# Down projection of a gated feed-forward block in 2x2 blocks with seven products, and its weights checked through an int8 copy

## The chip, the cores and the metric

The kernel runs on one core of a Trainium2 chip. The metric is device time in microseconds (us), lower is better. A core has a matrix engine (PE, with weight loads in its own row PEld), a vector engine (DVE), an activation engine (ACT), a general engine (POOL) and a queue engine (SP) that mostly issues transfers (DMA) between the chip's memory and the core's on-chip memory (SBUF). Matrix products are summed in eight banks (PSUM) of 128 x 512 float32 numbers each.

## The reference, cut to what matters

The kernel computes a transformer block with adaptive layer norms for 2 sequences of 1024 tokens, 1024 wide, in float32. The part that the change touches is the feed-forward block at the end, with 2752 inner channels. Its three weight matrices hold only -1, 0 and 1:

```python
def _L0_ffn_ref(x, Wg, Wu, Wd, ag, au, ad):
    gate = jnp.einsum('bsh,ih->bsi', x, Wg) * ag
    up = jnp.einsum('bsh,ih->bsi', x, Wu) * au
    h = jax.nn.silu(gate) * up
    out = jnp.einsum('bsi,hi->bsh', h, Wd) * ad
    return out
...
x = x + ga * _L0_attn_ref(...)
h = _layernorm(x, axis=-1) * (1 + cb) + sb
x = x + gb * _L0_ffn_ref(h, ...)
```

## The kernel before, in words

The stages follow each other: modulation vectors, QKV projections, attention, output projection (all of it until about 1409 us), then the **gate and up pass** (1409 to 2019 us), then the **down projection** (2019 to 2346 us) and a short tail. Below, n is a number of rows, P is 128, b the sequence, and D is 1024.

Precise products: the weights are small integers and exact, so only the token side is split into a rounded part `hi` and the rest `lo`, and each product is two passes over TensorE, `hi` and `lo`.

**Gate and up pass** (`gate_up`, from L1636). For each of two sequences it runs over 11 groups p of 256 inner channels (the last has 192). A group is multiplied in 2x2 blocks with seven products in place of eight: the tuple `SEVEN` (L768) names for each product e the output half (x or y: its PSUM bank), the left operand (a block or a sum S1 to S4 of blocks of the weights), the right one (of the tokens, `hs_tiles`, made earlier and resident), and the block sum to which it adds. A product is 8 matmuls 128x512 for gate and 8 for up; a group is 112 matmuls. Around them:
- `stage` (L1508) loads the weights of the next group into two buffers of the pool `wst`, four transfers of 512 KB on SP.
- `weight_operands` (L1602) makes the seven left operands: casts A11, A12, A22 on ACT (L1611, L1612, L1617) and four sums on POOL (L1613 to L1616).
- `ternary` (L1561) checks the raw weights with two DVE passes 2048 wide (L1570 counts entries that are neither what 0 or 1 gives, L1573 counts the -1), into `count_a` and `count_b`. Gate and up weights are checked once: in sequence 0 from group 1 on, group 0 in sequence 1.
- The down weights are checked on the way too (`down_checks`, L1634): a piece of 1 MB per group is loaded into a `wst` buffer (`wdst`), checked, and stored to `wd_dram`. One lies in the last group of sequence 0, ten in sequence 1.
- Products leave PSUM by an ACT copy (L1661), a DVE addition (L1666), `silu` on ACT (L1676) and the product with up on DVE (L1679). The activation goes to memory (`act_dram`) in pieces of 256 KB, four per group, on SP.
- At the start of sequence 1 its seven token operands are loaded (`tokens_in`, L1524: a 1 MB transfer through the two `traw` buffers, an ACT cast L1528, a DVE subtraction L1529), behind sequence 0's last uses.

From the second group on, PE follows the order of the program (`pinned`); other engines' orders are set by a scheduler, each engine executing its own queue in order. Checks stand behind the latest PSUM read (`hold`, L1554).

**Down projection** (from L1692). All weights (11 pieces) stay in SBUF, loaded at its start from `wd_dram` by SP's and ACT's queues (L1705). For each of 16 tiles of 128 tokens, an activation row block `a` is loaded on ACT's queue (L1713), cast to `hi` on ACT (L1722), and `lo` is the difference on DVE (L1723); two sets of these buffers alternate. 88 matmuls (22 channel blocks, hi and lo, two halves of the output) fill two banks; then DVE multiplies by the gate (L1742), POOL adds the residual `x1` (L1743), and SP stores. 1408 matmuls in all. Two probes (`exact`, L1577) and the `verdict` (L1342) stand in this stage: if the weights aren't what the fast path needs, a slow general path runs at the end.

Of the kernel before, what the change touches and what calls it, by code (L numbers as in the profile page):

```python
# [19 lines left out]
P = 128  # L20
# [460 lines left out]
def kernel(  # L481
# [35 lines left out]
    count_b = flag.tile([P, NCOUNT + 2], FP, name="count_b")  # L517
    nc.vector.memset(count_b, 0.0)
# [46 lines left out]
    wd_dram = [dram.tile([P, 2, D], FP, tag=f"wd_{p}", name=f"wd_{p}") for p in range(NPR)]  # L565
    act_dram = [dram.tile([P, NJ, 2, NIC, P], FP, tag=f"act_{b}", name=f"act_{b}") for b in range(B)]
# [775 lines left out]
    def verdict(pool, psp):  # L1342


        seen = pool.tile([P, NCOUNT + 2], FP, name="seen")
        nc.vector.tensor_sub(seen, count_a, count_b)
        total = pool.tile([P, 1], FP, name="total")
        nc.vector.tensor_reduce(total, seen, mybir.AxisListType.X, ALU.add)
        nc.vector.tensor_scalar(total, total, 0.0, None, ALU.is_equal)
        nc.vector.tensor_mul(total, total, fine)  # L1350
        lows = psp("lows")[0:1, 0:P]
        transpose(lows, total, ident)
        least = pool.tile([1, 1], FP, name="least")
        nc.vector.tensor_reduce(least, lows, mybir.AxisListType.X, ALU.min)
        bad = pool.tile([1, 1], FP, name="bad")
        nc.vector.tensor_scalar(bad, least, 1.0, None, ALU.is_lt)
        nc.vector.tensor_copy(bad_i, bad)
# [133 lines left out]
    def share(a):  # L1491
# [11 lines left out]
    stp, wsp, ptp = (  # L1503
        gu.enter_context(tc.tile_pool(name=n, bufs=k, side="right", reuse_waits="tile"))
        for n, k in (("wst", 2), ("wops", 1), ("fpart", 1))
    )

# [53 lines left out]
    def ternary(w, at, pool):  # L1561


        junk = pool.tile([P, 2048], mybir.dt.bfloat16, tag="junk", name=f"junk_{at}")
        n = w.shape[0]
        shape = list(w.shape[1:])
        j = junk[0:n, 0 : int(np.prod(shape))]
        if len(shape) > 1:
            j = j.rearrange("p (a b) -> p a b", a=shape[0])
        hold(nc.vector.scalar_tensor_tensor(  # L1570
            j, w, 0.0, w, ALU.is_gt, ALU.not_equal, accum_out=count_a[0:n, at : at + 1]
        ))
        hold(nc.vector.tensor_scalar(  # L1573
            j, w, -1.0, None, ALU.is_equal, ALU.add, accum_out=count_b[0:n, at : at + 1]
        ))

    def exact(t, at, bank, pool):  # L1577


        matmul(bank, ident_r, t, start=True, stop=True)  # L1580
        junk = pool.tile([P, 2048], mybir.dt.bfloat16, tag="junk", name=f"probe_{at}")[:, 0:512]
        nc.vector.scalar_tensor_tensor(
            junk, bank, 1.0, t.bitcast(FP), ALU.mult, ALU.not_equal, accum_out=count_a[:, at : at + 1]
        )

    if True:
# [10 lines left out]
        with gu:  # L1597
            W_ORDER = ("A11", "A12", "S2", "S1", "S3", "S4", "A22")

            token_tiles([5, 6])  # L1600

            def weight_operands(p, st, b):  # L1602
# [5 lines left out]
                W = {q: wsp.tile([P, 2, KC // 2, P], FR, tag=f"w{q}", name=f"w{q}_{b}_{p}") for q in W_ORDER}  # L1608
# [9 lines left out]
                if b == (p == 0):  # L1618
                    for kh in range(2):
                        v = st[kh].rearrange("p a k f -> p (a k) f")[:, :, 0 : 2 * n]  # L1620
                        ternary(v, 2 * p + kh, jkp)
                return W

            down_checks = ({NPR - 1: [0]}, {p: [p + 1] for p in range(NPR - 1)})

            def gate_up(b):
# [5 lines left out]
                for p in range(NPR):  # L1632
# [4 lines left out]
                    for p_ in down_checks[b].get(p, ()):  # L1637
                        r0, n = PAIRS[p_]
                        t = stp.tile([P, 2, D], FP, tag="wst", name=f"wdst_{p_}")
                        nc.sync.dma_start(t[0:n], wd_t[ds(r0, 2 * n), :].rearrange("(m p) e -> p m e", p=n))  # L1640
                        ternary(t[0:n].rearrange("p m e -> p (m e)"), 2 * NPR + p_, jkp)
                        nc.sync.dma_start(wd_dram[p_][0:n], t[0:n])
                    n = PAIRS[p][1]
                    if p + 1 < NPR or b + 1 < B:
                        st.append(stage((p + 1) % NPR))
                    bank = {(mat, c_): ffbank(f"{mat}{c_}_{b}_{p}") for mat in "gu" for c_ in "xy"}
                    part = {}
                    for e, (c_, qa, qb_, q) in enumerate(SEVEN):
                        done = {}
# [18 lines left out]
                        if q in QUAD:  # L1668
# [13 lines left out]
                            if q == "U6":  # L1682
                                last_read[0] = ins
                            nc.sync.dma_start(
                                act_dram[b][0:n, :, h, ib, :], u[0:n].rearrange("p (j t) -> p j t", j=NJ)
                            )
# [5 lines left out]
        with ExitStack() as dn:  # L1692
            aip = [own(dn, f"ain{i}") for i in range(2)]
            lop0, hip0, hip1, lop1, gbp = (own(dn, n) for n in ("alo0", "ahi0", "ahi1", "alo1", "gb"))
            wdp = [own(dn, f"wd{p}") for p in range(NPR)]
            xp1, yp = own(dn, "x1in", 2), own(dn, "yout", 2)
            hip, lop = (hip0, hip1), (lop0, lop1)
            dlp = jkp
            wd = [wdp[p].tile([P, 2, D], FR, tag=f"wd{p}", name=f"wd_{p}") for p in range(NPR)]
            gb = []  # L1700

            def more_wd(which):
                for p in which:
                    n = PAIRS[p][1]
                    (nc.scalar if 0 < p < 8 else nc.sync).dma_start(wd[p][0:n].bitcast(FP), wd_dram[p][0:n])  # L1705

            n1 = PAIRS[-1][1]
            for b in range(B):
                for j in range(NJ):
                    for h in range(2):  # L1710
                        t = 2 * j + h
                        a = aip[h].tile([P, NIC, P], FP, tag=f"ain{h}", name=f"a_{b}_{t}")
                        nc.scalar.dma_start(a[:, 0:WHOLE], act_dram[b][:, j, h, 0:WHOLE])  # L1713
                        nc.scalar.dma_start(a[0:n1, WHOLE:NIC], act_dram[b][0:n1, j, h, WHOLE:NIC])
                        hi = hip[h].tile([P, NIC, P], FR, tag="ahi", name=f"hi_{b}_{t}")
                        lo = lop[h].tile([P, NIC, P], FR, tag="alo", name=f"lo_{b}_{t}")
                        cuts = [0, 4, 10, WHOLE] if (b, t) == (0, 0) else [0, WHOLE]
                        for v in (
                            *((slice(0, P), slice(u, w)) for u, w in zip(cuts, cuts[1:])),
                            (slice(0, n1), slice(WHOLE, NIC)),  # L1720
                        ):
                            nc.scalar.copy(hi[v[0], v[1]], a[v[0], v[1]])  # L1722
                            nc.vector.tensor_sub(lo[v[0], v[1]], a[v[0], v[1]], hi[v[0], v[1]].bitcast(FP))  # L1723
                        if (b, t) == (0, 0):
                            more_wd(range(NPR))
                            for b_ in range(B):
                                gb.append(gbp.tile([P, D], FP, name=f"gb{b_}"))
                                nc.scalar.dma_start(gb[b_], gate_dram[5][b_].partition_broadcast(P))
                        pss = [ffbank(f"dn_{b}_{t}_{n}") for n in range(2)]
                        for ib in range(NIC):  # L1730
                            rows = PAIRS[ib // 2][1]
                            for s_, src_ in enumerate((hi, lo)):
                                for n in range(2):
                                    matmul(
                                        pss[n], src_[0:rows, ib, :], wd[ib // 2][0:rows, ib % 2, ts(n, HALF)],
                                        start=(ib == 0 and s_ == 0), stop=(ib == NIC - 1 and s_ == 1),
                                    )
                        x1 = xp1.tile([P, D], FP, tag="x1", name=f"x1_{b}_{t}")
                        nc.sync.dma_start(x1, x1_dram[b * NT + t])
                        y = yp.tile([P, D], FP, tag="y", name=f"y_{b}_{t}")  # L1740
                        for n in range(2):
                            nc.vector.tensor_mul(y[:, ts(n, HALF)], pss[n], gb[b][:, ts(n, HALF)])  # L1742
                            nc.gpsimd.tensor_add(y[:, ts(n, HALF)], y[:, ts(n, HALF)], x1[:, ts(n, HALF)])  # L1743
                            nc.sync.dma_start(out[b, ts(t, P), ts(n, HALF)], y[:, ts(n, HALF)])
                        if (b, t) == (0, 0):
                            for i, src_ in enumerate((hi, lo)):
                                exact(
                                    src_[:, 0:4].rearrange("p k t -> p (k t)"), NCOUNT + i, ffbank(f"probe{2 + i}"), dlp
                                )
                        if (b, t) == (1, 2):  # L1750
                            verdict(dlp, ffbank)


# [51 lines left out]
```

## Time and profile before

| What | us |
| --- | --- |
| median of 3 runs (2354.20 to 2360.12) | 2358.19 |
| the profiled execution's own time | 2356.1 |
| its span | 2354.4 |
| PE busy | 2198.6 |
| DVE busy | 1266.9 |
| POOL busy | 886.8 |
| ACT busy | 841.8 |
| gate and up pass, first matmul to first of down | about 1409 to 2019 |
| down projection, first matmul to last | 2019.36 to about 2345.9 |

How to read it: the span is that of the profiled execution, all times within it count from its start. PE is busy 93% of it, so time goes where PE waits or where it has less to do. PE's records overlap by their pipelining; the distance of their starts is what a matmul costs. "PEclk" is the clock granted to PE (1.00 is full). The mean granted clock of this execution was 0.979.

### The profile page before, as it was taken

The numbers are of one execution on the slowest core, as the hardware profiler recorded it, in microseconds if no ns is written. First come the engines' busy times: TensorE is split into PE (matmuls) and PEld (weight loads), VectorE is DVE, ScalarE is ACT, GpSimd is POOL, SyncE is SP. The second block draws the span as 40 slices with busy tenths as digits, with TensorE's granted clock in tenths as the row PEclk, the third lists the DMA queues.
The fourth block names the chain that finished last, engine by engine and source line by source line (L and its number), as shares of the span: only waits on it lengthen the run. The fifth ranks groups of instructions, "written<-read, shape, count | busy, mean of one in ns | idle before, by whom it ended". The sixth has DMA issues, their size and how long they took to land.

```text
span 2354.4 us, 26878 instructions
## 1 busy us (share of the span) xinstructions
PE 2198.6 (93%) x9713; PEld 1211.6 (51%) x9713; DVE 1266.9 (54%) x1820; ACT 841.8 (36%) x1701; POOL 886.8 (38%) x679
## 2 busy tenths in 40 slices
PE   6999999999999998798888797999989999999998
PEld 2444443333333332232222245888767788788887
DVE  5775752456556343366765566667785454322221
ACT  1322224444444445465555224333343333211110
POOL 2330202442336455666575653344343342011111
PEclk9999999999999999999999998999999999999999
DMA  9887777346246323754532466433476656833331
GB/s 368 307 305 274 287 269 242 133 135 221 94 155 217 134 90 141 209 166 130 153 117 90 127 201 219 128 114 117 131 267 214 201 182 198 334 126 126 124 104 38
DMA packets 264034, 423.18 MB, mean 180 GB/s; under 512 B 12940, under 2 KB 198604, under 8 KB 250132
## 3 DMA queue, kind: packets, MB, share of 16 engines
q1 hardware_dynamic: 256048, 382.00, 48.7%
q10 hardware_dynamic: 7844, 39.37, 4.6%
q8 instruction: 79, 1.29, 0.2%
q14 instruction: 63, 0.52, 0.1%
HBM read 290.51 MB, written 130.81 MB: 179 GB/s over the span
## 4 chain that ended last, share of the span: by engine, by line
PE 30%; DVE 7%; issue 7%; DMA 4%; POOL 3%; ACT 1%; SPq 0%; DVEq 0%; POOLq 0%; ACTq 0%
PE dn L742 12%; PE ux L742 4%; PE gx L742 4%; PE uy L742 4%; PE gy L742 3%; PE bank L742 2%; DVE junk L1570 2%; DVE p L1106 1%; DMA wst<-in_L_ffn_Wu_dram 1%; DMA wd<-wd 1%; DVE junk L1573 1%; PE sc L742 1%; DMA traw<-hs 1%; ACT p L1074 1%; PE av L742 1%
## 5 line engine op out<-in xcount | busy, mean ns | idle before, releaser
L1074 ACT ACTIVATE p<-sc,kw 128x128 f32<-128x128 f32 (+3 forms) x1024 | 422.6, 514 | 394.7 <-PE sc L742 374.9
L742 PE MATMUL bank<-wT,a 128*128 128x512 f32 x768 | 365.8, 610 | 14.5 <-ACT P L966 8.0
L1106 POOL TENSOR_TENSOR p<-p,p 128x1024 f32<-128x1024 f32 (+3 forms) x128 | 263.6, 2060 | 238.9 <-PE av L742 209.2
L1106 DVE TENSOR_TENSOR p<-p,p 128x1024 f32<-128x1024 f32 (+3 forms) x192 | 235.9, 1243 | 141.7 <-POOL p L1078 75.5
L742 PE MATMUL bank<-wB,a 128*128 128x512 f32 x576 | 270.3, 605 | 1.9 <-DVE raw L973 1.4
L742 PEld LDWEIGHTS bank<-wT,a 128*128 128x128 f32 x768 | 136.7, 191 | 199.0 <-issue 166.5
L742 PE MATMUL dn<-wd,hi 128*128 128x512 f32 (+1 forms) x704 | 218.4, 391 | 2.5 <-DMA wd<-wd 2.5
L742 PE MATMUL sc<-cq,ck 32*128 32x512 f32 (+3 forms) x1536 | 185.2, 543 | 37.5 <-ACT p L1074 28.7
L742 PE MATMUL dn<-wd,lo 128*128 128x512 f32 (+1 forms) x704 | 218.0, 391 | 1.0 <-DVE lo L1723 1.0
L1078 POOL TENSOR_SCALAR_AFFINE_SELECT p<-p 128x256 f32<-128x256 f32 x256 | 130.5, 522 | 187.0 <-ACT p L1074 177.5
L742 PE MATMUL av<-p,cv 128*32 128x512 f32 (+3 forms) x1536 | 169.9, 507 | 13.9 <-POOL p L1078 13.9
L742 PEld LDWEIGHTS bank<-wB,a 128*128 128x128 f32 x576 | 102.1, 189 | 145.8 <-issue 125.1
L1613 POOL TENSOR_TENSOR wS<-wst,wst 128x1024 fp32r<-128x1024 f32 (+1 forms) x22 | 53.5, 2430 | 304.2 <-DMA wst<-in_L_ffn_Wu_dram 213.9
L1743 POOL TENSOR_TENSOR y<-y,x 128x512 f32<-128x512 f32 x32 | 40.8, 1293 | 316.1 <-DVE y L1742 316.1
L742 PEld LDWEIGHTS dn<-wd,hi 128*128 128x128 f32 (+1 forms) x704 | 132.6, 189 | 30.9 <-DMA wd<-wd 3.0
L742 PEld LDWEIGHTS sc<-cq,ck 32*128 32x128 f32 x1536 | 62.8, 185 | 166.0 <-issue 97.9
L742 PEld LDWEIGHTS dn<-wd,lo 128*128 128x128 f32 (+1 forms) x704 | 132.6, 188 | 29.7 <-DVE lo L1723 1.5
L1742 DVE TENSOR_TENSOR y<-dn,gb 128x512 f32<-128x512 f32 x32 | 20.6, 686 | 209.0 <-issue 196.6
L1722 ACT CAST hi<-a 96x256 fp32r<-96x256 f32 (+4 forms) x34 | 42.5, 1300 | 247.3 <-PE dn L742 223.4
L742 PEld LDWEIGHTS av<-p,cv 128*32 128x32 f32 x1536 | 32.5, 109 | 140.7 <-issue 78.3
L742 PE MATMUL gy<-hs,wS 128*128 128x512 f32 (+1 forms) x352 | 91.4, 402 | 7.8 <-DVE gP L1666 5.3
L742 PE MATMUL uy<-hs,wS 128*128 128x512 f32 (+1 forms) x352 | 91.0, 401 | 6.4 <-DVE uP L1666 6.4
(224 smaller groups left out, 3298.0 us busy)
## 6 DMA issues: line engine op xcount, KB each, us to landing
a<-hop SPq DMA_DIRECT2D x20, 1792.0 KB
wm<-in_L_wmod_dram SPq DMA_DIRECT2D x48, 512.0 KB
wB<-in_L_attn_Wqkv_dram SPq DMA_DIRECT2D x21, 1024.0 KB
wst<-in_L_ffn_Wg_dram SPq DMA_DIRECT2D x40, 512.0 KB
wst<-in_L_ffn_Wu_dram SPq DMA_DIRECT2D x40, 512.0 KB
a<-act ACTq DMA_DIRECT2D x16, 1280.0 KB
qk<-qs SPq DMA_DIRECT2D x16, 1024.0 KB
hop<-a SPq DMA_DIRECT2D x8, 1792.0 KB
```

The lines of the kernel that those rows point to most:

```text
L742: return in_order(nc.tensor.matmul(*args, **kw_))
L1074: last_exp[0] = nc.scalar.activation(p[:, g, lo:hi], sp[:, g, lo:hi], AF.Exp, bias=kw[:, d, h_ : h_ + 1])
L1078: last_mask[0] = nc.gpsimd.affine_select(out=p[:, :, 0:P], in_=p[:, :, 0:P], pattern=[[0, 2], [1, P]], compare_op=ALU.is_ge, fill=0.0, bas ...
L1106: adders[b](half, jb).tensor_add(dst, dst, ps[half][:, :, 0:n])
L1570: hold(nc.vector.scalar_tensor_tensor(j, w, 0.0, w, ALU.is_gt, ALU.not_equal, accum_out=count_a[0:n, at : at + 1]))
L1573: hold(nc.vector.tensor_scalar(j, w, -1.0, None, ALU.is_equal, ALU.add, accum_out=count_b[0:n, at : at + 1]))
L1613: nc.gpsimd.tensor_add(f["S1"], raw["A21"], raw["A22"])
L1722: nc.scalar.copy(hi[v[0], v[1]], a[v[0], v[1]])
L1742: nc.vector.tensor_mul(y[:, ts(n, HALF)], pss[n], gb[b][:, ts(n, HALF)])
L1743: nc.gpsimd.tensor_add(y[:, ts(n, HALF)], y[:, ts(n, HALF)], x1[:, ts(n, HALF)])
```

## The change: what it does

- **Down projection in 2x2 blocks with seven products.** Rows are token tiles (two of each pair), columns the halves of the output, and the inner dimension is the channel pair of a group. It goes operand by operand: for each sequence, for each of the seven products, over 4 pairs of token tiles; each of these 56 steps is 22 matmuls (11 groups, hi and lo). Each step loads its left operand (0.72 MB) from memory into a ring of four `lo` buffers, casts it into one of three `hi` buffers on ACT, and subtracts in place on DVE. Weights of a product (2.88 MB) come in four pieces, one per step, two products ahead. Two products share one place, so these two are loaded for both sequences. All these loads, the residual's and the stores are on SP's queue. Partial sums go from PSUM to SBUF and back as in the gate pass.
- **Sums in the gate pass.** Each group makes the four sums S1 to S4 of its activations (S1, S2 on DVE, S3, S4 on POOL, 128x512) and stores seven operands in place of four.
- **Down weights' sums** in 11 groups (sequence 0: p = 2, 4, 6, 8, 10; sequence 1: p = 1, 2, 4, 5, 7, 8): a load of 1 MB into a `traw` buffer, the check, four POOL subtractions 128x512, seven stores of 256 KB in place of one of 1 MB.
- **The check**: an int8 copy on ACT and one DVE pass that counts where the copy differs, in place of two DVE passes. Its buffer is doubled. The probes stand in the last group of the gate pass, on one of its token operands.
- `wops` becomes one pool for each operand, and the gate pass's next weights are issued ahead of the down weights' load.

```diff
-    stp, wsp, ptp = (
+    W_ORDER = ("A11", "A12", "S2", "S1", "S3", "S4", "A22")
+    stp, *wsp, ptp = (
...
-        for n, k in (("wst", 2), ("wops", 1), ("fpart", 1))
+        for n, k in (("wst", 2), *((f"w{q}", 1) for q in W_ORDER), ("fpart", 1))
...
-    def ternary(w, at, pool):
...
+    def small_integers(w, at, pool):
...
+        small = pool.tile([P, 2048], mybir.dt.int8, tag="junk", bufs=2, name=f"junk_{at}")
...
+        nc.scalar.copy(j, w)
         hold(nc.vector.scalar_tensor_tensor(
-            j, w, 0.0, w, ALU.is_gt, ALU.not_equal, accum_out=count_a[0:n, at : at + 1]
+            j, j, 0.0, w, ALU.add, ALU.not_equal, accum_out=count_a[0:n, at : at + 1]
         ))
-        hold(nc.vector.tensor_scalar(
-            j, w, -1.0, None, ALU.is_equal, ALU.add, accum_out=count_b[0:n, at : at + 1]
-        ))
...
-            down_checks = ({NPR - 1: [0]}, {p: [p + 1] for p in range(NPR - 1)})
+            down_at = {
+                **{(0, 2 * p + 2): p for p in range(5)},
+                **{(1, p): i + 5 for i, p in enumerate((1, 2, 4, 5, 7, 8))},
+            }
...
+            def down_parts(p, t):
+                n = PAIRS[p][1]
+                small_integers(t[0:n].rearrange("p m e -> p (m e)"), 2 * NPR + p, jkp)
...
+                v = right["raw"][1].tile([P, 4, HALF], FP, tag="traw1", name=f"wdsum_{p}")
+                nc.gpsimd.tensor_sub(v[:, 0], b12, b11)
+                nc.gpsimd.tensor_sub(v[:, 1], b22, v[:, 0])
+                nc.gpsimd.tensor_sub(v[:, 2], b22, b12)
+                nc.gpsimd.tensor_sub(v[:, 3], b21, v[:, 1])
+                for q, src in (("B11", b11), ("B21", b21), ("B22", b22), *((f"T{i + 1}", v[:, i]) for i in range(4))):
+                    nc.sync.dma_start(wdt_dram[:, OTHERS.index(q), p], src)
...
                     for e, (c_, qa, qb_, q) in enumerate(SEVEN):
+                        if e == 3 and wdst is not None:
+                            down_parts(p_, wdst)
...
+                            if q_ != "A21":
+                                keep_act(q_, u)
+                            else:
+                                act_sum("S1", nc.vector, "tensor_add", "A21", "A22")
+                                act_sum("S3", nc.gpsimd, "tensor_sub", "A11", "A21")
+                                act_sum("S2", nc.vector, "tensor_sub", "S1", "A11")
+                            if q_ == "A12":
+                                act_sum("S4", nc.gpsimd, "tensor_sub", "A12", "S2")
...
+            def operand_in(s):
...
+                b, e, j = STEPS[s]
+                lo = rings[f"lo{s % 4}"](s)
+                hi = rings[f"hi{s % 3}"](s)
+                load(lo.bitcast(FP), act_dram[b][:, e, j])
+                nc.scalar.copy(hi, lo.bitcast(FP))
+                nc.vector.tensor_sub(lo, lo.bitcast(FP), hi.bitcast(FP))
...
+            for s, (b, e, j) in enumerate(STEPS):
...
+                operand_in(s + 3)
+                nxt = OTHERS[e + 2] if b == 0 and e < 5 else {(1, 0): "B21", (1, 2): "T4"}.get((b, e))
+                if nxt is not None:
+                    weights(nxt, b, [j])
+                residual_in(s + 2)
+                for dst, src in stores:
+                    nc.sync.dma_start(dst, src)
...
+                for k_ in range(NPR):
+                    for l in range(2):
+                        matmul(
+                            bank, left[l][:, k_, :], wd[qb_][:, k_],
...
+                if q in ("P1", "U2", "P5"):
+                    part[j, q] = (late_parts if q == "U2" else early_parts)[j](f"{q}_{b}")
+                    nc.scalar.copy(part[j, q], bank)
+                    continue
+                m, h = QUAD[q]
+                if q == "U6":
+                    y = early_parts[j](f"{q}_{b}")
+                    nc.vector.tensor_mul(y, gate[b][:, ts(h, HALF)], bank)
+                else:
+                    y = part[j, MATE[q]]
+                    nc.vector.tensor_add(y, y, bank)
+                    nc.vector.tensor_mul(y, y, gate[b][:, ts(h, HALF)])
+                nc.gpsimd.tensor_add(y, y, x1_of.pop(s))
+                stores.append((out[b, ds((2 * j + m) * P, P), ts(h, HALF)], y))
```

## The prediction

> **What bounds the kernel now.** I read the slices of the page first, then the stages' windows, then who waited for whom, then the chain of waits at the end. The slices show PE busy nearly throughout; the last 14 of 40 (59 us each) are the gate and up pass and the down projection:
>
> ```profile
> PE   6999999999999998798888797999989999999998
> DMA  9887777346246323754532466433476656833331
> ```
>
> Windows from group 2 of sequence 0 on: sequence 0, the change of sequence, sequence 1, down. Columns: length, busy us with instructions of PE, PEld, DVE, ACT, POOL, granted clock, DMA share, GB/s.
>
> ```profile
> 1460.00:1721.00 261.00, 258.22 (x1127) 207.34 (x1126) 188.41 (x187) 95.16 (x133) 96.80 (x38) 1.00 0.44 132
> 1721.00:1758.00 37.00, 28.98 (x114) 23.09 (x113) 32.57 (x27) 16.86 (x17) 17.37 (x6) 0.91 0.76 263
> 1758.00:2019.40 261.40, 256.50 (x1121) 206.40 (x1121) 129.93 (x136) 89.99 (x130) 90.57 (x38) 1.00 0.65 210
> 2019.40:2346.00 326.60, 322.90 (x1412) 265.45 (x1410) 87.69 (x77) 41.38 (x33) 38.27 (x30) 0.99 0.37 132
> ```
>
> PE bounds all four: what is not PE work is about 3 us, 8 us, 5 us and 4 us. The waits of PE between 1460 and 2020 say which engines they came from (total, times, longest):
>
> ```profile
> PE uy L742 <- DVE uP L1666: 6.4, 10, 3.6
> PE gy L742 <- DVE gP L1666: 5.3, 2, 4.4
> PE ux L742 <- ACT uU L1661: 3.1, 3, 1.5
> PE gy L742 <- ACT gP L1661: 0.8, 1, 0.8
> ```
>
> That is 15.6 us. The chain from 2000 us on (start, us, what) is PE but for the start of down and the tail:
>
> ```profile
> 2014.45 12.20 DMA wd<-wd
> 2026.67 9.38 DMA wd<-wd
> ...
> 2045.75 200.01 PE dn L742 x880
> ...
> 2245.87 66.20 PE dn L742 x292
> ```
>
> A matmul of down costs 66.20 / 292 = 0.2267 us; a slower engine there hides behind PE. So fewer matmuls in down are time, one for one, if the operands arrive.
>
> **Down, part 1: matmuls.** 1408 become 56 x 22 = 1232. At 0.2267 us that is 279.3 us. Before, the stage took 2345.74 - 2019.36 = 326.4 us: 319.2 of matmuls, 0.5 of probes, waits of 1.03 and 2.54, and about 3 of slow clock behind the second. Removed: 47.1 us, before new losses.
>
> **Down, part 2: the start.** Step 0 needs its operand and the first product's weights; all come on SP, behind the last group's stores of S3, S4 and A22, which wait for POOL and DVE. ACT's queue no longer helps. The first load of 0.72 MB, by the 1 MB traw load (5.5 to 6.5 us), takes about 4 to 5, then cast and subtraction. Early places (lo0, hi0) come free before the pass ends, so part of this is hidden. Bounds: 0, and the old start's loss of 6.7 us. I take 4 (the old row is nearest: the same resource is late).
>
> What a short wait does to the clock is in the rows of the old start:
>
> ```profile
> 2032.93 0.61 PE L742 MATMUL dn<-wd,lo 128*128 128x512 f32 x2
> 2036.09 0.73 PE L742 MATMUL dn<-wd,hi 128*128 128x512 f32 x2 [2.54 <-DMA wd<-wd]
> 2036.65 1.02 PE L742 MATMUL dn<-wd,lo 128*128 128x512 f32 x2
> 2037.47 1.05 PE L742 MATMUL dn<-wd,hi 128*128 128x512 f32 x2
> ```
>
> After 2.54 us of waiting, pairs take 1.02 to 1.05 in place of 0.61 for some 3 us; so I charge a wait of this length double. The Trainium skill, "TensorE: Matmul & The Clock Gate", Part 1 (the HAM clock gate), says that the clock halves after about one idle window of 3.4 us; by it waits under 3.4 us would be charged once and my start would be about 2.5 in place of 4. The trace decides for the double charge.
>
> **Down, part 3: the supply.** A step lasts 22 x 0.2267 = 4.99 us. ACT casts 128x1408: from 128x2560 at 2.34 us, 1.29. DVE subtracts: from 3.76 us (2.8 at the quickest), 1.55 to 2.07. With a PSUM copy of 0.6 or addition of 0.7 and a product, each stays below 4 of 4.99 us; POOL has 1.29 per step. All these have cover, about 1 us of it per step; without it a step would show the excess, up to 56 x 1. Bytes: 56 x 0.72 = 40.4 MB of operands, 9 x 2.88 = 26.0 of weights, 8.4 of residual, 8.4 of output, 83 MB in about 283 us: 294 GB/s on average, where the old stage moved 132. The worst steps (products 1 and 4 of sequence 0: operand, weights, residual and store) ask 1.97 MB in 4.99 us, 393 GB/s. What the queues can do shows where their share is full:
>
> ```profile
> 2019.30:2026.00 6.70, 5.67 (x25) 4.35 (x25) 3.95 (x5) 1.81 (x3) 0.00 (x0) 1.00 1.02 415
> 2026.00:2033.00 7.00, 7.00 (x33) 5.79 (x32) 0.00 (x0) 0.00 (x0) 0.00 (x0) 1.00 1.04 344
> 2033.00:2040.00 7.00, 4.46 (x13) 3.21 (x12) 0.00 (x0) 0.00 (x0) 0.00 (x0) 0.76 1.04 405
> ```
>
> 344 to 415 GB/s. At 415 nothing is late; at 344 each worst step takes 5.73, 0.74 over, 8 steps: 6 us, less what the rings of three steps ahead catch. I take 2, bounds 0 and 6. The Trainium skill, "DMA: Bandwidth & Descriptors", Specifications, speaks against the change here: 358 GB/s from memory per core. By it the worst steps would be 0.5 over, 4 us in place of 2 in the sum; the rows of 405 and 415 lie above that figure. Down together: -47.1 + 4 + 2 = -41.
>
> **Tail.** After the last matmul one half is scaled (0.70) and added (1.05 to 1.29) in place of two: -1, between -1.3 and 0.
>
> **Gate pass, work that moves off PE's path.** Rows (mean ns of one):
>
> ```profile
> L1570 DVE SCALAR_TENSOR_TENSOR junk<-wst 128x2048 bf16<-128x2048 f32 x20 | 59.8, 2991 | 0.3
> L1573 DVE TENSOR_SCALAR_CACHE_REDUCE junk<-wst 128x2048 bf16<-128x2048 f32 x20 | 45.6, 2281 | 0.3
> L1528 ACT CAST hs<-traw 128x2048 fp32r<-128x2048 f32 x7 | 13.3, 1903 | 5.9 <-DMA traw<-hs 5.9
> ```
>
> A group is 112 x 0.2267 = 25.4 us. Per group of sequence 0: DVE has two checks of 5.3 us each; one pass of each goes, S1 and S2 come (the SBUF additions of 128x512 took 1.27): about 18 to 16 us. ACT gets two int8 copies, 1.9 each by the cast's row (9.1 to 12.9), with a down piece 14.8. POOL gets S3, S4 (2 x 1.29) and, with a down piece, four more (5.2): 10 to 17.8. No engine is full; this is hidden while nothing stands in the wrong place in a queue. DMA: each group has three more stores of 256 KB; one with a down piece in sequence 0 also a load of 1 MB and seven stores: 3.7 MB, 144 GB/s on top of 132. A full share there is 132 / 0.44 = 300 GB/s, so such a group stands at 0.92, every second one: covered, but loads then land nearer to sequence 1's 7.2 us than to 5.0.
>
> **Gate pass, waits.** Three old ones shrink. (1) Sequence 0: the 8 or so waits of DVE's checks ahead of the PSUM additions, 2 to 3 us: -2 (bounds -3, 0). (2) Change of sequence: group 0 took 36.9 us in place of 25.4; waits 4.42 and 3.60 behind L1570 and L1573, and slow clock. Half the check passes go, but four int8 copies come on ACT, the new down piece of the last group holds both traw buffers through which the tokens come, and that transfer chain (6.5 us a piece) stays. -3.5; bounds -11.5 and +5 (one more piece late). (3) Sequence 1: 0.85 + 0.76 + 1.47 + 0.73 + 0.90 = 4.7, where gate's weights queue behind the down piece in the same pool; they don't share it any more: -4.7 (0 if they wait for another reason).
> A new one comes. POOL runs its queue in order: the next group's four weight sums (10.6 us), T1 to T4, then S3, S4 of the activations. In a group with a down piece S4 ends some 7 us into the next group. SP is in order too: the store of S4 waits, and behind it the loads of the weights after next (issued at about +7.4, before at the start of the group or earlier). They land 5.0 us later in sequence 0: +12.4. On ACT the casts wA11, wA12 (2 x 1.05) and an int8 copy (1.9) stand ahead of the PSUM copies of U2, without which product 4 can't start at +14.5: 12.4 + 4.0 - 14.5 = 2. Bounds 0 (the copies stand first) and 4.4 (the longest wait seen; 4.2 if the loads take 7.2). Five groups: +10. In sequence 1 the nearest rows are the waits of 0.73 to 1.47 above, of the same form (late weights, then casts before a PSUM copy): 1 x 6 groups: +6, bounds 0 and 2.6 each. Gate together: -2 - 3.5 - 4.7 + 10 + 6 = **+6**.
>
> **Sum.** 2356.1 (the profiled execution's own time, 2.1 below the median of the runs shown) - 41 - 1 + 6 = **2320 us**.
>
> **Rivals.**
> (a) *Everything hides.* The rings start early, POOL's sums come in time, the 15.6 us of waits go: 2356.1 - 47 - 1 - 15.6 = 2292. For it: no engine but PE is above 73% in the two passes' windows. Against: SP and POOL in order.
> (b) *The weights come late after every down piece.* 11 waits of 3.6 (the second longest seen, in place of 2 and 1): 39.6 - 10 = +30, 2344; at 4.4 each, 2353. For it: one queue now carries everything. Against: the other groups recover.
> (c) *Down becomes bound by its transfers*, and slower. Place: the 56 operand loads and 36 weight pieces on SP's single queue, each waiting for a ring place that PE must free. It decides where the stage's rate falls below 83 MB / 326 us = 255 GB/s. Price: at the 210 GB/s of sequence 1's pass, which also issues on SP between waits, 396 us, +69: 2356.1 + 69 - 1 + 6 = 2430. For it: the old stage moved 132 at an easy pace and nobody has asked 294 for long in this half of the span (250 over 2000 to 2100 us is the most). Against: full-share rows of 344 and more, and three steps (15 us) of lead over a load of about 5.
> (d) *It doesn't do what it says*: the count isn't zero, and the general path runs too; at least the whole feed-forward part again (over 900 us). int8 holds -1, 0, 1 and the comparison is of values, so little speaks for it.
>
> **How the numbers follow.** Forecast (2300 to 2341) 0.58; (a) 0.14; (b) 0.13; (c) 0.13; (d) 0.02. The range 2290 to 2352 takes in (a) but its lowest part, and (b) but its end; left out are (c), (d) and about 0.05. A difference below 0.3% (7 us) is about what a measurement here can't tell from none. Faster: 0.58 + 0.14 + 0.09 of (b) = 0.81; same: 0.03 of (b) and 0.01 of (c), 0.04; slower: the rest, 0.15.
>
> **What would show it.** Right: down from first to last matmul 280 to 288 us, matmuls still 0.227 apart, DMA share above 0.75 there; change of sequence 31 to 36 us; in groups after a down piece waits of 1 to 3 us behind ACT's copies, with the weights' loads behind S4's store. Wrong: steps longer than 5 us throughout down with PE waiting for lo; or the gate pass above 625 us.

## The result, and the profile after

The changed kernel takes 2378.23 us (median of 4 runs, 2375.25 to 2382.64) where the kernel before took 2356.46 beside it: a ratio of 1.0092, 95% interval 1.007 to 1.0115. It is slower by 22 us; 2320 was forecast. The profiled execution has a span of 2373.5 us, 19.1 above the one of before.

The page's slices of the changed kernel:

```profile
PE   6999999999999997898888787899899899999998
PEclk9999999999999998899999897999998999999999
DMA  9887877246347315654532576555658666598765
GB/s 368 307 310 259 300 271 251 101 134 237 112 135 229 143 49 192 176 154 130 147 115 86 143 230 208 191 168 161 196 183 258 209 219 199 179 373 320 276 230 180
```

In the kernel before, the clock line of the same page was:

```profile
PEclk9999999999999999999999998999999999999999
```

PE is lower in some slices of the gate and up pass (25 to 35), and its clock with it, not in those of down; the differences ahead of slice 25 come to 2.9 us in all. The windows of its stages say it plainly: groups 1 to 10 of sequence 0, the first group of sequence 1, the other ten, down (columns as in the prediction):

```profile
1466.76:1762.60 295.84, 266.64 (x1122) 211.43 (x1120) 191.89 (x167) 137.44 (x156) 183.86 (x83) 0.95 0.58 185
1762.60:1807.76 45.16, 34.49 (x113) 25.88 (x112) 34.25 (x27) 17.51 (x19) 25.46 (x8) 0.77 0.70 233
1807.76:2086.32 278.56, 263.58 (x1125) 212.64 (x1124) 139.47 (x144) 103.86 (x137) 152.52 (x85) 0.97 0.66 211
2086.32:2365.60 279.28, 279.28 (x1232) 230.90 (x1231) 128.13 (x111) 84.96 (x77) 65.49 (x33) 1.00 0.78 281
```

Down is PE from end to end: 1232 matmuls in 279.4 us (the first starts at 2086.16, just ahead of the last window), full clock, no wait, with 281 GB/s moving beside it. Cuts by the starts of matmuls in both traces give where 19 us come from:

| Stretch | before, us | after, us | difference |
| --- | --- | --- | --- |
| start to the pass's first matmul | 1408.84 | 1411.71 | +2.9 |
| group 0, sequence 0 | 52.19 | 55.05 | +2.9 |
| groups 1 to 10, sequence 0 | 259.93 | 295.84 | +35.9 |
| group 0, sequence 1 | 36.85 | 45.16 | +8.3 |
| groups 1 to 10, sequence 1 | 261.55 | 278.40 | +16.9 |
| down, first matmul to the end of the last | 326.51 | 279.44 | -47.1 |
| tail | 8.51 | 7.87 | -0.6 |

The first row isn't the change's: this start lies between 1406.2 and 1419.5 in the profiles of this study. The second row is: this group takes 54.3 to 55.3 us in every kernel with the changed down projection, and 51.7 with the new check alone (run 9). PE waits there for a subtraction on DVE, and S1 and S2 (0.69 and 1.64 us) now stand ahead of it. What the change saved in down it lost 1.4 times over in the pass ahead, 674.4 us in place of 610.5. There, the waits of PE in the changed kernel (1460 to 2380; total, times, longest):

```profile
PE gx L740 <- ACT gU L1697: 40.7, 12, 6.7
PE gx L740 <- DVE hs L1527: 15.1, 4, 5.9
PE ux L740 <- ACT uP L1697: 2.8, 4, 0.8
```

The old 11.7 us behind DVE's additions are nearly gone (0.9 is left); in their place PE waits 40.7 us at product 4 (gx, S3; products are counted from 0) for ACT's copy of U2. The 15.1 us behind `hs` lie in group 0 and at the change of sequence. A wait costs more than its length: the group that starts at 1519.49 waits 7.1 us and takes 36.25 in place of 25.4, for the clock drops after the wait.

That group is worth reading engine by engine; the two other groups of sequence 0 above 30 us repeat it. ACT (start, length, idle time before and its releaser):

```profile
1528.89 0.58 ACT L1697 COPY uP<-ux 128x512 f32<-128x512 f32 x1 [6.75 <-POOL aS L1673]
...
1538.41 1.04 ACT L1605 CAST wA<-wst 128x1024 fp32r<-128x1024 f32 x1 [6.04 <-DMA wst<-in_L_ffn_Wu_dram]
1539.36 1.89 ACT L1568 CAST junk<-wst 128x2048 int8<-128x2048 f32 x1
1541.16 0.58 ACT L1697 COPY gU<-gx 128x512 f32<-128x512 f32 x1
```

and the matmul that it released:

```profile
1541.88 3.75 PE L740 MATMUL gx<-hs,wS 128*128 128x512 f32 x8 [6.25 <-ACT gU L1697]
```

The copy needs nothing that wasn't there at about 1531; it stands third in ACT's queue, behind a cast that waits for weights. SP shows why these come late:

```profile
1532.18 0.36 SPq L1667 DMA_DIRECT2D act<-aS  x1
1532.64 0.45 SPq L1512 DMA_DIRECT2D wst<-in_L_ffn_Wg_dram  x1
```

The load follows the store of S4 by half a microsecond, 13 us into the group. POOL had these two sums to make, S3 and S4, and DVE was at the checks:

```profile
1525.52 3.33 POOL L1673 TENSOR_TENSOR aS<-uP,uU 128x512 f32<-128x512 f32 x1
1528.82 3.34 POOL L1673 TENSOR_TENSOR aS<-uU,aS 128x512 f32<-128x512 f32 x1
```

```profile
1523.89 3.82 DVE L1569 SCALAR_TENSOR_TENSOR junk<-junk,wst 128x2048 int8<-128x2048 int8 x1
...
1527.64 3.36 DVE L1569 SCALAR_TENSOR_TENSOR junk<-junk,wst 128x2048 int8<-128x2048 int8 x1
```

Each POOL sum ends 1.2 us after a DVE pass has ended: it seems to take its own time of 1.3 us only once DVE lets go, which run 7 tests.

### The profile page after: what moved, and what is told of

The parts are those of the page before. It is cut to its first block, busy times and chain, and to the rows that moved or that the text cites. A ratio compares the mean times of both kernels' runs of the same rounds, so it can differ in the third digit from the quotient of the medians.

```text
span 2373.5 us, 27195 instructions
## 1 busy us (share of the span) xinstructions
PE 2181.8 (92%) x9537; PEld 1193.2 (50%) x9537; DVE 1326.1 (56%) x1842; ACT 944.8 (40%) x1780; POOL 1072.6 (45%) x776
## 4 chain that ended last, share of the span: by engine, by line
PE 29%; POOL 7%; DVE 6%; DMA 5%; issue 4%; ACT 2%; SPq 0%; POOLq 0%; DVEq 0%; ACTq 0%
PE dx L740 7%; PE dy L740 5%; PE gx L740 4%; PE ux L740 4%; DMA wst<-in_L_ffn_Wu_dram 3%; PE gy L740 3%; PE uy L740 3%; PE bank L740 2%; POOL aS L1673 1%; DVE p L1104 1%; PE sc L740 1%; DMA wdst<-in_L_ffn_Wd_dram 1%; ACT p L1072 1%; POOL wS L1610 1%; DVE aS L1673 1%
## 5 line engine op out<-in xcount | busy, mean ns | idle before, releaser
L740 PE MATMUL gx<-hs,wS 128*128 128x512 f32 (+1 forms) x352 | 102.3, 436 | 48.9 <-ACT gU L1697 40.7
L1785 DVE TENSOR_TENSOR lo<-lo,hi 128x1408 fp32r<-128x1408 f32 x56 | 95.1, 1702 | 91.6 <-ACT hi L1784 91.5
L1607 POOL TENSOR_TENSOR wS<-wst,wst 128x1024 fp32r<-128x1024 f32 (+1 forms) x22 | 51.7, 2348 | 191.3 <-DMA wst<-in_L_ffn_Wu_dram 126.6
L1784 ACT CAST hi<-lo 128x1408 fp32r<-128x1408 f32 x56 | 76.9, 1374 | 128.3 <-DMA lo<-act 84.1
L1848 POOL TENSOR_TENSOR early_P<-early_P,x1in 128x512 f32<-128x512 f32 x16 | 38.4, 2400 | 164.4 <-DVE early_P L1847 159.6
L740 PEld LDWEIGHTS gx<-hs,wS 128*128 128x128 f32 (+1 forms) x352 | 71.4, 207 | 71.6 <-issue 45.4
L1702 DVE TENSOR_TENSOR gP<-gP,gx 128x512 f32<-128x512 f32 (+1 forms) x22 | 15.1, 687 | 164.6 <-PE gx L740 107.8
L740 PE MATMUL gx<-hs,wA 128*128 128x512 f32 (+1 forms) x352 | 91.2, 402 | 11.4 <-DVE hs L1527 10.3
L740 PE MATMUL ux<-hs,wS 128*128 128x512 f32 (+1 forms) x352 | 95.5, 416 | 2.8 <-ACT uP L1697 2.8
```

What stands on the lines that cost most here:

```text
L740: return in_order(nc.tensor.matmul(*args, **kw_))
L1607: nc.gpsimd.tensor_add(f["S1"], raw["A21"], raw["A22"])
L1702: last_read[0] = nc.vector.tensor_add(t[0:n], t[0:n], ps[0:n])
L1784: nc.scalar.copy(hi, lo.bitcast(FP))
L1785: nc.vector.tensor_sub(lo, lo.bitcast(FP), hi.bitcast(FP))
L1848: nc.gpsimd.tensor_add(y, y, x1_of.pop(s))
```

## The experiments

All times stand beside runs of the kernel before on the same chip (2358.7 to 2361 us); a gain against the changed kernel is the difference of the two ratios, 0.01 being 23.6 us. "Groups" are lengths between starts of groups, 25.39 us without a wait.

**1. The order on ACT alone.** A helper puts the casts A11 and A12 and the int8 copies behind the last PSUM copy of P5:

```diff
-        nc.scalar.copy(j, w)
+        after_copy(nc.scalar.copy(j, w))
...
-                nc.scalar.copy(f["A11"], raw["A11"])
-                nc.scalar.copy(f["A12"], raw["A12"])
+                after_copy(nc.scalar.copy(f["A11"], raw["A11"]))
+                after_copy(nc.scalar.copy(f["A12"], raw["A12"]))
```

> The changed kernel with one order on ACT: the casts A11 and A12 of the next group's weights and the int8 copies stand behind the PSUM copies of P5 of the group in progress. Theory 1 (order on ACT): PE waits in the gate and up pass because ACT, which works in order, meets the cast of weights still on their way and then an int8 copy ahead of the PSUM copies of U2; with the order turned, the waits of product 4 behind ACT's copy (40.7 us) go and the groups of sequence 0 return to 25.4 to 26.5 us: about 2320 us. Theory 2 (late supply): the weights themselves come too late, behind POOL's sums and the store of S4 on SP; then the wait only moves to the start of the next group, and the gain is below 15 us: 2363 or more.

Measured: 2360.24 us, ratio 0.9995 (0.9981 to 1.0009). 23 us gained, less than half of what theory 1 asked. The waits at product 4 are gone, and new ones stand at product 2, behind the copy of P1:

```profile
PE ux L740 <- ACT uP L1703: 30.5, 9, 5.9
```

P1's copy overwrites a buffer that the sum S3 still has to read, and now also queues behind the late casts. The order is one cause; the supply is late as well. Neither theory stands alone.

**2. The old check in the changed kernel** (two DVE passes, no int8 copy).

> The changed kernel with the old check: two DVE passes, no int8 copy. Everything else as changed. Theory 1: without the copies ACT's order around the casts is that of the kernel before (the U2 copies right at the cast), so most of the 40.7 us of waits go, while DVE's longer checks hold the weight buffers longer: 2315 to 2340 us. Theory 2 (late supply): a check of two passes holds the buffers longer, loads come later: as slow as the changed kernel or slower, 2375 or more.

Measured: 2386.53 us, 1.0113 (1.0096 to 1.013). Theory 1 missed by 45 us or more: without int8 copies ACT's order was as before, and the loss stayed (5 us more by the ratios, within the intervals). The cheaper check isn't what costs; run 9 tests it alone.

**3. Stores of S3 and S4 behind the next weights' loads on SP.**

```diff
-                        if q != "A21":
-                            keep_act(q, act[q])
+                        if q in ("S3", "S4") and p + 1 < NPR:
+                            late.append(lambda k=keep_act, q=q, t=act[q]: k(q, t))
+                        elif q != "A21":
+                            keep_act(q, act[q])
...
+                    while late:
+                        behind(late.pop(0)(), last_stage[0])
```

> The changed kernel with the stores of the activations' sums S3 and S4 issued on SP behind the loads of the next weights in place of ahead of them. Theory 1: little, at most 10 us, since the DVE check frees the weight buffer only about 1 us before the store of S4 is issued: 2368 to 2378 us. Theory 2 (SP blocked by the store of S4): the loads are issued earlier by several us in every group, 30 us or more are gained: below 2348 us.

Measured: 2343.51 us, 0.9932 (0.9915 to 0.9948): 38 us, theory 2's size. The loads of the group that corresponds to the one above, now 8 us into it in place of 13:

```profile
1522.21 0.37 SPq L1514 DMA_DIRECT2D wst<-in_L_ffn_Wg_dram  x1
1522.63 0.50 SPq L1514 DMA_DIRECT2D wst<-in_L_ffn_Wu_dram  x1
1525.50 0.37 SPq L1514 DMA_DIRECT2D wst<-in_L_ffn_Wg_dram  x1
```

Theory 1's reason, that the check frees the buffer only 1 us ahead of S4's store, holds for the second of the two weight buffers alone. The first one's check pass ended at 1527.7 in the changed kernel, 4.9 us before its load was issued behind the store. In this run each load follows the end of its own check pass (1522.05 and 1525.35), though S4 itself ends about as late as before, at +12.3. Sequence 0's groups fall to 25.4 to 28.5; sequence 1 keeps three of 30.8 to 32.4.

**4. Without the four sums of down weights.**

```diff
-                nc.gpsimd.tensor_sub(v[:, 0], b12, b11)
-                nc.gpsimd.tensor_sub(v[:, 1], b22, v[:, 0])
-                nc.gpsimd.tensor_sub(v[:, 2], b22, b12)
-                nc.gpsimd.tensor_sub(v[:, 3], b21, v[:, 1])
```

> The changed kernel without the four POOL sums of the down weights; the stores take raw blocks in their place, so the bytes stay and the output of the down projection is not the reference's. Theory 1: POOL frees the weights and makes the activations' sums some 6 us earlier in groups with a down piece, but ACT's order stays, and in sequence 0 the DVE check still holds the buffer: 10 to 20 us gained, 2358 to 2368. Theory 2b (POOL is the one that makes everything late): the waits of the groups after a down piece go, 40 us or more: below 2338 us.

Measured: 2334.34 us, 0.9882 (0.9856 to 0.9908): 50 us with the same bytes. Sequence 1's groups are all between 25.4 and 26.3, sequence 0's at 25.4 to 30. So it isn't the bytes; POOL's queue is the place. In sequence 1 these four sums, with the stores that wait for them, are nearly the whole loss: S3 and S4 run without a check of gate's and up's weights beside them there and take 1.3 to 1.8 us. The change of sequence (45.4) has another reason.

**5. S3 and S4 on DVE in place of POOL.**

> The changed kernel with the activations' sums S3 and S4 made on DVE in place of POOL. Theory now (POOL, slowed by DVE): in the changed kernel a POOL sum of 128x512 takes 1.3 us by itself, 3.3 us beside the DVE checks and up to 9.5 us at the change of sequence, and what waits for it is the store on SP with the weights' loads behind it and the PSUM copy of P1 (its target is what S3 reads). With S3 and S4 on DVE all of that goes but POOL's sums of down weights: the groups of sequence 0 at 25.5 to 28 us, the change of sequence below 40: 2325 to 2340 us. Rival (ACT's order alone): the waits behind ACT's copies stay as the casts still stand there: above 2360 us.

Measured: 2345.51 us, 0.9947 (0.9927 to 0.9966); the rival is out, 5 us less than expected came. Change of sequence: 37.9 in place of 45.2. What remains are 4.7 to 5.5 us behind ACT's copy in three groups of sequence 1 (T1 to T4 still stand in POOL's queue, as run 4 has it, and ACT's casts still stand first), and 1.7 to 2.9 behind DVE in four groups of sequence 0.

**6. Both: S3 and S4 on DVE, their stores late.**

> S3 and S4 on DVE, and their stores behind the next weights' loads on SP as in the run before. If what the late store gained (35 us) was only the wait for POOL's S4, it adds little to the sums on DVE: within 5 us of that kernel. If the place on SP matters by itself, 10 us or more below it. Expected 2320 to 2335 us.

Measured: 2341.29 us, 0.9933 (0.9909 to 0.9957), 4 below run 5 and within the intervals: the late store had mainly got round POOL's slow S4. The range expected was missed by 6.

**7. Without the DVE pass of gate's and up's check.**

> The changed kernel without the DVE pass of the check of gate's and up's weights (the ACT int8 copy stays; those weights are not checked). Two things go with it: DVE's two-input passes beside POOL's sums, and the hold on the weight buffers until their end. POOL theory: POOL's 128x512 sums fall to 1.3 to 1.8 us in sequence 0 and the 10 us of every second group there mostly go, about 35 us, while sequence 1 keeps its waits: 2335 to 2350 us. Rival (T sums and bytes make it late whatever DVE does): 2365 or more.

Measured: 2359.95 us, 0.9999 (0.9988 to 1.0011), between the two. POOL's S4 in sequence 0, in the changed kernel and then in this one (mean ns of one in the last column but one):

```profile
L1673 POOL TENSOR_TENSOR aS<-uU,aS 128x512 f32<-128x512 f32 x9 | 29.7, 3302 | 14.6 <-DVE uU L1715 14.6
```

```profile
L1675 POOL TENSOR_TENSOR aS<-uU,aS 128x512 f32<-128x512 f32 x9 | 11.6, 1291 | 14.6 <-DVE uU L1717 14.6
```

So DVE's passes do stretch POOL's sums, from 1.29 to 3.30. The time followed by 22 us only: the change of sequence fell to 38.1, sequence 0 gained 12. ACT's order had changed with the shorter check, and four groups of sequence 0 waited 2.9 to 4.6 us for the copy of P1; ACT in this run:

```profile
1533.96 1.90 ACT L1568 CAST junk<-wst 128x2048 int8<-128x2048 f32 x1 [8.84 <-DMA wst<-in_L_ffn_Wu_dram]
1535.77 1.04 ACT L1613 CAST wA<-wst 128x1024 fp32r<-128x1024 f32 x1
1536.71 0.58 ACT L1699 COPY gP<-gx 128x512 f32<-128x512 f32 x1
```

Here it is an int8 copy that waits 8.84 us for weights, ahead of PSUM copies. The theory of what slows POOL held, the time that I put on it didn't.

**8. All three: sums on DVE, late stores, order on ACT.**

> S3 and S4 on DVE, their stores behind the next weights' loads, and the casts of the next weights behind the PSUM copies of P5 on ACT: all three together. The down projection saves 47 us against the kernel before; if the gate and up pass comes back to some 15 us above its 610 us, this is 2310 to 2325 us, faster than both kernels. If the supply of weights is late still, the wait moves to the next group's start or to the copies of P1 and the time stays above 2335.

Measured: 2317.54 us (2316.47 to 2319.54), 0.9827 (0.9808 to 0.9847): 43 us below the kernel before beside it, faster than both. Its waits (1463 to 2330) and its stages:

```profile
PE gy L740 <- DVE gP L1717: 11.4, 5, 4.1
PE ux L740 <- ACT uP L1710: 4.3, 3, 2.1
PE gx L740 <- DVE hs L1529: 3.5, 2, 2.5
PE ux L740 <- DVE uP L1717: 1.0, 1, 1.0
```

```profile
1464.50:1732.40 267.90, 259.27 (x1122) 209.14 (x1121) 197.28 (x187) 137.91 (x157) 137.41 (x64) 0.99 0.66 206
1732.40:1768.60 36.20, 28.61 (x113) 22.53 (x112) 29.93 (x28) 18.29 (x19) 12.03 (x4) 0.91 0.78 250
1768.60:2027.00 258.40, 254.50 (x1120) 206.92 (x1119) 161.35 (x164) 104.36 (x137) 131.36 (x65) 1.00 0.72 231
2027.00:2306.50 279.50, 279.50 (x1234) 231.42 (x1233) 130.07 (x114) 85.00 (x77) 61.89 (x31) 1.00 0.80 281
```

Sequence 1 loses 4 us, the change of sequence as much as before the change, sequence 0 some 14.

**9. The new check alone, in the kernel before.**

> The kernel before with the new check alone (int8 copy on ACT and one DVE pass), its down projection and down checks as they were. Theory now: the check alone does little harm, since POOL has no sums of activations or down weights there and SP no store behind them: DVE's waits (11.7 us of the 15.6) shrink, ACT's order gives some back: 2345 to 2360 us. Rival (the int8 copies on ACT are the loss): 2370 or more.

Measured: 2354.65 us, 0.9982 (0.9972 to 0.9993). Sequence 0's groups are at 25.38 to 25.39 but for one (25.77; before: 25.4 to 26.7), so half the passes do end DVE's waits there; the rival is out.

**10 and 11. The order on ACT with one of the other two**: with the late stores, S3 and S4 on POOL (10); with the sums on DVE, the stores in their place (11).

> The changed kernel with the order on ACT and the late stores of S3 and S4, but S3 and S4 still on POOL. If POOL's slow sums matter only through the store on SP, this equals the kernel with all three (2317). Theory now: the PSUM copy of P1 still waits for S3 to be read by POOL (waits of 4 to 6 us at product 2 in the run with the order alone), and the change of sequence stays near 44 us: 2328 to 2345.

> The changed kernel with the order on ACT and S3 and S4 on DVE, their stores in the old place on SP. With the sums on DVE the stores wait for nothing long, so the place on SP should add little: 2315 to 2325 us. If the place matters by itself: 2330 or more.

Measured: 2341.24 us, 0.9929 (0.9912 to 0.9945), with the change of sequence at 44.8 and waits for P1's copy of up to 4.0 as theory said; and 2329.21, 0.9871 (0.9845 to 0.9898), 4 above what I expected. So with the sums on DVE and the order turned the place on SP counts for some 10 us, by intervals that just part; without the order it was 3, within them. Together, as ratios to the kernel before:

| | S3, S4 on POOL | S3, S4 on DVE |
| --- | --- | --- |
| as changed | 1.0092 | 0.9947 |
| late stores | 0.9932 | 0.9933 |
| order on ACT | 0.9995 | 0.9871 |
| both | 0.9929 | 0.9827 |

The three aren't additive: late stores gain 38 us alone, DVE 34, the two together 38; the order gains 23 alone, nothing on top of the late stores, and 25 on top of both.

**12. Down pieces mostly in sequence 1** (two in sequence 0, nine in a row), all else as in run 8.

```diff
-                **{(0, 2 * p + 2): p for p in range(5)},
-                **{(1, p): i + 5 for i, p in enumerate((1, 2, 4, 5, 7, 8))},
+                (0, 8): 0, (0, 10): 1,
+                **{(1, p): p + 1 for p in range(1, NPR - 1)},
```

> All three, and the down weights' pieces moved: two in sequence 0 (groups 8 and 10), nine in sequence 1 (groups 1 to 9). In sequence 0 three of five groups lose their third DVE check and the waits of 1.4 to 2.6 us behind it: about 7 us there. In sequence 1 POOL has the four weight sums and four sums of down weights in every group, 17 us of 25.4, and SP the most bytes. If POOL and the transfers carry that: 2308 to 2314 us; if not, waits of 2 us and more in each group of sequence 1: 2325 or more.

Measured: 2328.57 us, 0.9874 (0.9857 to 0.989), the worse of the two cases. Sequence 0 lies at 25.4 to 25.8 but for one group of 27.4; in sequence 1 the first three groups are free, the next six take 27.2 to 30.8, with waits of 1.5 to 3.6 for P1's copy. A group carries one piece; nine running pile up a delay.

## Why the prediction was wrong, point by point

- *Down, part 1* (1232 matmuls of 0.2267, 47.1 us removed): right, 279.4 us.
- *Down, part 2 and 3* (+4 at the start, +2 for supply): both were 0. No wait stands in the stage, though the first 59 us ran at a DMA share of 0.97 and 371 GB/s. The lateness of SP's queue that I had charged at the start was covered.
- *Rival (c)*, down bound by its transfers: out. It needed less than 255 GB/s; the stage moved 281 on average. In the slice of 59 us around its start the core moved 373 GB/s without a wait of PE, above the 358 that the Trainium skill, "DMA: Bandwidth & Descriptors", Specifications, states as the limit of each of two cores on one memory; this kernel runs on one core.
- *Tail* (-1): right, -0.6.
- *Gate pass, the old waits* (1), (2), (3): those of (1) went (in the run of the check alone, all), those of (3) were replaced by others; (2), the change of sequence, went the other way, 45.2 us in place of 31 to 36. Most of it is a POOL sum of 9.54 us that held P1's copy, and with it ACT's token casts, for 8.55 us: with the sum on DVE it is 37.9, without the check passes beside it 38.1. Group 0 of sequence 0 had no term and lost 2.9.
- *Gate pass, the new wait*: **this step failed.** "In a group with a down piece S4 ends some 7 us into the next group ... 12.4 + 4.0 - 14.5 = 2 ... Five groups: +10 ... 1 x 6 groups: +6". The place was right: store of S4, loads behind it, casts and int8 copy ahead of U2's copies, in the groups after a down piece. The size was not. In sequence 0 S4 ended at +12.7 in place of +7, the loads landed at +18.9, and three groups waited 6.2 to 6.7 us, which cost 9 to 11 with the slow clock. In sequence 1 four groups waited 3.0 to 5.0 us in place of 1, which cost 5 to 8. Three terms were missing: POOL's sums stand still while DVE runs a two-input pass (S3 and S4 took 6.7 us in place of 2.6, which is 4.1 of the 5.7 that S4 was late); the slow clock raises the price of a wait (7.1 us of waits cost 10.9 in the group above); and S3's input buffer is P1's target, so POOL holds ACT's queue too. Late weights also make POOL's next sums late (they begin at +16 in place of +14.8 in the group of a down piece), but the long groups of sequence 0 don't grow, 36.3, 35.5 and 34.6 us, and no run isolates this. The whole pass came to +64 in place of +6, beyond the 625 us that I had named as a sign of being wrong.
- *Rival (b)* had this mechanism, at +30. Its 39.6 us of waits come near the 40.7 measured behind ACT's copies of U2, partly by chance, for these range from 0.3 to 6.7. What it lacked is a charge for the clock, although my own row of the start of down had shown the doubling, and the change of sequence, which was 12 us off.
- A slip without effect: the two stages fill the last 16 or so of the 40 slices, not 14.

The causes are shown by runs 1, 3, 4 and 5, each of which takes one link out. The edits of 1, 3 and 5 together (run 8) bring back the forecast, 2317.5 for 2320, but by other terms: the old waits of the pass are replaced by new ones, and down starts without the loss that I had charged. That it fits the forecast so closely is luck. Not separated: how much of run 4's gain is POOL's time by itself and how much its DVE neighbours.

## What to carry to other kernels

Adding work to an engine that is 40% busy isn't free when its results stand in another engine's in-order queue: write down, for each added instruction, who queues behind its store and whose buffer it still reads. When a stage prepares the next group's inputs, a delay of one link can come round again (in run 12 three groups were free and the next six late); add the clock that each wait costs. Here the saved matmuls were worth 47 us, and three placements (sums on the engine that makes their inputs, stores behind loads, casts behind PSUM copies) decided whether they were seen.

## What the runs showed of the hardware

- POOL gives way to DVE's two-input passes in SBUF. At the change of sequence a sum of 128x512 took as long as DVE's row of passes beside it:

```profile
1768.24 9.54 POOL L1673 TENSOR_TENSOR aS<-uP,uU 128x512 f32<-128x512 f32 x1 [4.69 <-DVE uU L1715]
```

  DVE's last pass of that row ended at 1776.6, and the sum 1.1 us later; ACT's copy of P1, which waited for it, stood for 8.55 us. Without such passes the sum takes 1.29. A pass with one input in SBUF does no such thing: in run 2, S4 ran beside the old check's second pass in 1.27 us.

```profile
1530.69 2.27 DVE L1575 TENSOR_SCALAR_CACHE_REDUCE junk<-wst 128x2048 bf16<-128x2048 f32 x1
1531.24 1.27 POOL L1679 TENSOR_TENSOR aS<-uU,aS 128x512 f32<-128x512 f32 x1
```

  The Trainium skill, "GPSIMD Engine Reference", Specifications, says that POOL shares its SBUF interfaces with VectorE and that instructions with two SBUF inputs contend; the trace agrees and gives the size, 3.3 to 9.5 us in place of 1.29. DVE pays less or nothing: a check pass takes up to 3.82 in place of 2.28, and the two beside the sum of 9.54 us took 2.28.
- Waits of 6.2 to 6.7 us were followed by eight matmuls in 3.40 to 3.75 us in place of 1.98, waits of 2.6 to 3.1 by eight in 2.6 to 3.2, one of 1.57 by 2.08. The granted clock of the pass in sequence 0 fell to 0.95 from 1.00.
- 281 GB/s over 279 us, in transfers of 256 to 768 KB on one queue, cost TensorE nothing.
